# Softmax reciprocals by way of HBM, a planner that serves transfers in turn, and a finer last tail, in a 32-graph GNN kernel

## The chip, the cores and the metric

The program runs on one core of a Trainium2 chip. The metric is the device time of one execution in microseconds (us), lower is better; three executions of the kernel before are known, and one more under the profiler.

## The reference

There are 32 independent graphs of 512 nodes with 256 features and a dense 512 x 512 adjacency matrix each. Every graph goes through four layers, and each layer ends with `x = layernorm(x + layer(x))`:

- **Layer 0**, attention with 8 heads of 32 features: `q, k, v = x@Wq+bq, x@Wk+bk, x@Wv+bv`; `scores = q k^T / sqrt(32)`, set to -9e15 where `adj` is not positive; `softmax` over the keys; `attn @ v`; `@ Wo + bo`.
- **Layer 1**: `h = (1+eps) x + adj@x`, then `relu(h@W1+b1)@W2+b2` with 512 hidden features.
- **Layer 2**: `eps x + adj@x`, `@W1+b1` with 1024 hidden features, RMS norm, silu, `@W2+b2`.
- **Layer 3**: a layer norm with gamma and beta, a degree-normalised Laplacian `L = I - D^-1/2 adj D^-1/2`, `softplus(xn@W_self + L@xn@W_neigh)`.

All of it is in float32. The division of the softmax by its row sums is what the first part of the change is about: for each head and each query there is one row sum, and the attention output (features on the partitions, queries along the free dimension) has to be multiplied by its reciprocal.

## The kernel before, in words

**Tiles.** P is 128 partitions and NT = 4 row tiles make one graph. Two groups `g` of four heads each (HPG = 4) are worked on at a time. For each row tile `t` TensorE (PE) writes four score matrices to `sc` (L779); VectorE (DVE) adds the mask and takes the row minimum (L803); ScalarE (ACT) takes exp and adds up the row sums `rs` (L817); DVE transposes the 1 MB tile `pq` in 32 x 32 blocks (L853); four DMAs carry it to a scratch tensor `via` in HBM (L865) and one carries it back as `pT`, now fully transposed (L877). After four tiles PE multiplies by `v` (L895, `po_att`), and the result goes to `oT`.

**The softmax reciprocals** (`normalise`, stage `rinv`). DVE takes the reciprocal of the 128 x 32 row sums into `rv` (L954). `split` turns it into three bf16 parts (three casts L919, two subtractions L926), PE transposes the parts (`pm_t`, L936), DVE or ACT copies the result to `mT` (L943, L944), and for each head group four bf16 matmuls with the 0/1 selector `sel_r` write the reciprocals, spread over the 32 features of each head, to the PSUM bank `pr_r` (L965). DVE multiplies `oT` by it (L976). `split` is used a second time for the RMS norm of layer 2 (`pb`, L1316).

**The dense stages** after it are `po<-wo` (L993), `ph` (aggregation, L1172), `pa` and `pg` (first dense layers, L1189), `po<-w` (second dense layers, L993), `pz` (L1438) and `pa_l` (Laplacian, L1480). The aggregated rows are held in `hT`, a tile with one buffer; the tag `xT`, with one buffer too, holds `xT` and later in the same graph `xnT` (the transposed input of layer 3). `adjT` has two buffers, `pq` two, `pT` four. `xT`, `adjT` and `xnT` are loaded from HBM in blocks with 128-byte pieces (`load_blocks`, L590) and finished by a DVE transpose (L677, L624, L1423). The last graph takes PE transposes for `xnT` and works in two halves (`row_tiles`).

**The order.** Nothing is left to queues at run time: every operation of all 32 graphs is put into a list with its engine, a cost in ns, what it reads and writes and which buffers it takes; `Order.run` plays a list scheduler over it and `Order.emit` issues the instructions of each engine in the order found. At each step the engine whose next operation could start first goes, and of the operations that it could start within 100 ns the one with the smallest key goes: `b * PERIOD + due + LEAD[stage]`, where `due` is a time from a schedule of one graph alone and LEAD a hand-set shift for each stage; the last graph has `HASTE` taken off. All DMAs go through SyncE's queue (SP), which issues in that order and waits in order. Before the change the planner lets a DMA take its cost from its own issue on, however many others are under way:

```
free[e] = o.t1 - self.TAIL[e] if e != "SP" else t + way[3].get("issue", 100)
```

so that SP is taken for the `issue` time alone, and the costs are long (6500 and 7500 ns for the 1 MB to and from `via`, 4900 for one of four `xT` blocks, 5800 for one of four `adjT` blocks).

**The end of the last graph** (stage `softplus`): softplus is computed as max(z,0) + ln(1 + exp(-|z|)). For each half ACT takes |z| (L1515), exp (L1520, after a table load) and ln (L1533, after a table load); DVE adds; the layer norm and the store follow.

Of the kernel before, what the change touches and what calls it, by code (L numbers as in the profile page):

```python
# [9 lines left out]
F32 = mybir.dt.float32  # L10
BF16 = mybir.dt.bfloat16
AF = mybir.ActivationFunctionType
ALU = mybir.AluOpType
# [3 lines left out]
P = 128  # L17
# [2 lines left out]
RMS_EPS = 1e-6  # L20
HEADS = 8

PERIOD = 63146
LEAD = {
    "adjT": 62300, "agg1": -7100, "agg2": -126300, "degree": 48800, "diag": 69400, "lap": -8500,
# [4 lines left out]
}  # L30


# [27 lines left out]
class Order:  # L60
# [9 lines left out]
    TABLE, TABLE_DUE = 1300, 9000  # L70

    TURN = {"whole": 93, "row": 290, "col": 150}
    TURN_DUE = 1750
    LATE = 0.17
    HASTE = -6727

    def __init__(self):
        self.ops = []
# [29 lines left out]
    def run(self, ops, key, back=False):  # L108
# [22 lines left out]
        table, turn = [None], ["whole"]  # L131

        pool_busy, dve_busy = [0.0, 0.0], [0.0, 0.0]

        def add(o):
            for i, way in enumerate(o.ways):
# [18 lines left out]
        while len(out) < len(ops):  # L155
# [67 lines left out]
                    if lst[i][2] is o:  # L223
                        del lst[i]
            o.t0, o.t1, o.way = t, t + cost, way
            free[e] = o.t1 - self.TAIL[e] if e != "SP" else t + way[3].get("issue", 100)
            end = o.t1 + way[3].get("lat", self.LAT[e])
            for x in o.bufs:
                if not x.taken:
# [53 lines left out]
def kernel(  # L283
# [68 lines left out]
        return sel  # L352

    NX = 2 * NT * HPG
    sel_r = selector(NX, HD, "sel_r")
    sel_t = selector(NT, P, "sel_t")


# [11 lines left out]


    def setup(engine, cost, fn, r=(), w=()):
        order.op(-1, [(engine, cost, fn, {"issue": cost})], r, w, (), None)

    def load(name, t, src, kb):
        setup("SP", max(560, kb * 2.8), lambda: nc.sync.dma_start(t, src), (), [(name,)])

    def load_w(w, name):
        k, m = w.shape
# [21 lines left out]
    def load_x(b, t):  # L401
        nc.sync.dma_start(t(), x[b].rearrange("(t p) d -> p t d", p=P))

    def load_adj(b, t):
        nc.sync.dma_start(t(), adj[b].rearrange("(t p) j -> p t j", p=P))
# [102 lines left out]
    def graph(b):  # L508
# [60 lines left out]
        def small(name, bufs=2, shape=None):  # L569
            return Buf(sb, shape or [P, NT], F32, "s_" + name, f"{name}_{b}", bufs)  # L570
# [3 lines left out]
        y = tmp([P, NT, D], "y_att", 2)  # L574
        ad = Buf(sb, [P, NT, N], F32, "adj_sb", f"adj_{b}", 1)
        op(
            [("SP", 4000 if first else 8100, lambda: load_x(b, y), {"issue": 1500 if first else 560, "lat": 300})],
            [], [(y, t) for t in range(NT)],
        )
        op(  # L580
            [("SP", 6000 if first else 8900, lambda: load_adj(b, ad), {"issue": 3000 if first else 560, "lat": 300})],
            [], [(ad, t) for t in range(NT)],
        )

# [9 lines left out]
        if early:  # L594
            for m in range(NT):
                pt = bank("pt_adj")

                def tr_adj(m=m, pt=pt):
                    for t in range(NT):
                        nc.tensor.transpose(  # L600
                            pt[:, t * P : (t + 1) * P], ad[:, t, m * P : (m + 1) * P], ident
                        )

                pe(
                    460, tr_adj, [(ad, t) for t in range(NT)],
                    [(pt,), ("began", m)], adjT, d_out,
                )
                act(
                    675,
                    lambda m=m, pt=pt: nc.scalar.activation(  # L610
                        adjT[:, m, :], pt(), AF.Identity, accum_out=d_out[:, m : m + 1]
                    ),
                    [(pt,)], [(adjT, m), (d_out, m)],
                )
        else:
            for q in range(4):
                op(
                    [("SP", 5800, lambda q=q: load_blocks(adjT(), adj[b], q), {"issue": 1250, "lat": 300})],
                    [("began", m) for m in range(NT)], [(adjT, m, q) for m in range(NT)],
                )  # L620
            for m0 in range(0, NT, 2):
                dve(
                    1200,
                    lambda m0=m0: nc.vector.transpose(  # L624
                        adjT[:, m0 : m0 + 2].rearrange("p m i -> p (m i)"),
                        adjT[:, m0 : m0 + 2].rearrange("p m i -> p (m i)"),
                    ),
                    [], [(adjT, m, q) for m in range(m0, m0 + 2) for q in range(4)]
                    + [(adjT, m) for m in range(m0, m0 + 2)],
                )  # L630
            for m in range(NT):
                act(
                    675,
                    lambda m=m: nc.scalar.activation(
                        adjT[:, m, :], adjT[:, m, :], AF.Identity, accum_out=d_out[:, m : m + 1]
                    ),
                    [], [(adjT, m), (d_out, m)],
                )
# [30 lines left out]
        else:  # L669
            for q in range(4):  # L670
                op(
                    [("SP", 4900, lambda q=q: load_blocks(xT(), x[b], q), {"issue": 660, "lat": 300})],
                    [("begun", c) for c in range(DC)], [(xT, c, q) for c in range(DC)],
                )
            dve(
# [89 lines left out]
        def attend(g):  # L765
# [5 lines left out]
            for t in range(NT):  # L771
# [78 lines left out]
                else:  # L850
# [12 lines left out]
                    def away(pq=pq, via=via):  # L863
                        for i in range(4):
# [3 lines left out]
                            )  # L868

                    op(  # L870
                        [("SP", 6500, away, {"issue": 2240, "lat": 300})],
                        [(pq, j) for j in range(HPG)], [(via,)],
                    )
                    op(
                        [(
                            "SP", 7500,
                            lambda pT=pT, via=via: nc.sync.dma_start(  # L877
                                pT().rearrange("p i j c s -> p (i j c s)"),
                                via().rearrange("a p i e -> (a p) (i e)"),
                            ),  # L880
                            {"issue": 600, "lat": 300},
                        )],
                        [(via,)], [(pT, a) for a in range(4)],
                    )
# [62 lines left out]

        def normalise():

            stage[0] = "rinv"  # L950
            rv = small("rv", 2, [P, NX])
            dve(
                240,
                lambda: nc.vector.reciprocal(rv(), rs().rearrange("p g t j -> p (g t j)")),  # L954
                [(rs, g, t, j) for g in range(2) for t in range(NT) for j in range(HPG)],
                [(rv,)],
            )
            mT = split(rv, NX, "sums")
            for g in range(2):
                pr_r = bank("pr_r")  # L960

                def spread(g=g, pr_r=pr_r):
                    for t in range(NT):
                        x = (g * NT + t) * HPG
                        nc.tensor.matmul(  # L965
                            pr_r[:, t * P : (t + 1) * P],
                            lhsT=sel_r[0 : 3 * NX, x : x + HPG].rearrange("p j e -> p (j e)"),
                            rhs=mT[0 : 3 * NX],
                            start=True,
                            stop=True,  # L970
                        )

                pe(240, spread, [(mT,)], [(pr_r,)])
                dve(
                    700,
                    lambda g=g, pr_r=pr_r: nc.vector.tensor_tensor(  # L976
                        oT[:, g, :], pr_r(), oT[:, g, :], ALU.mult
                    ),
                    [(pr_r,)], [(oT, g)],
                )  # L980

        def pair_sum(lhs, lhs_k, w, w_k, nk, y, step):
# [418 lines left out]
        else:  # L1401
            x3d = Buf(dr, [N, D], F32, "x3d", f"x3d_{b}", 2)
            op(
                [(
                    "SP", 6000,
                    lambda: nc.sync.dma_start(
                        x3d().rearrange("(t p) d -> p t d", p=P), x3()
                    ),
                    {"issue": 560, "lat": 300},
                )],  # L1410
                [(x3, t) for t in range(NT)], [(x3d,)],
            )
            for q in range(4):
                op(
                    [(
                        "SP", 4900, lambda q=q: load_blocks(xnT(), x3d(), q),
                        {"issue": 660, "lat": 300},
                    )],
                    [(x3d,)], [(xnT, c, q) for c in range(DC)],
                )  # L1420
# [83 lines left out]
        for rt in row_tiles:  # L1504
# [6 lines left out]
            s_ = lambda part=part: sp[:, part]  # L1511
            z_ = lambda part=part: zy[:, part, 0:D]
            x_ = lambda part=part: x3[:, part]
            act(
                cost, lambda s_=s_, z_=z_: nc.scalar.activation(s_(), z_(), AF.Abs), z0,  # L1515
                spk + [("sp", b)],
            )
            act(
                cost,
                lambda s_=s_: nc.scalar.activation(s_(), s_(), AF.Exp, scale=-1.0), [], spk,  # L1520
                table="exp",
            )

            dve(
                100 + 275 * n,
# [13 lines left out]
        for rt in row_tiles:  # L1539
            part = slice(rt[0], rt[-1] + 1)  # L1540
            op(
                [(
                    "SP", 3000,
                    lambda part=part: nc.sync.dma_start(
                        out[b].rearrange("(t p) d -> p t d", p=P)[:, part], sp[:, part]
                    ),
                    {},
                )],
                [(sp, t) for t in rt], [("out", b, rt[0])],
            )  # L1550
# [45 lines left out]
```

## Time and profile before

| | |
|---|---|
| median of 3 runs | 3408.11 us |
| lowest and highest | 3400.85 and 3408.37 us |
| the profiled execution's own time | 3402.63 us |
| its span, first to last instruction | 3400.9 us |
| granted TensorE clock | 0.993 |
| PE busy | 3305.0 us (97%) |
| DVE, ACT, POOL busy | 2751.4 (81%), 1897.9 (56%), 843.0 (25%) us |
| DMA queue of SP | 673.71 MB, packets 73.1% of 16 engines' span |

Busy times are sums over one core. Matmuls are pipelined and their modelled ends overlap, so PE's time for a step is read from the chain of waits (what released what, in order of time) rather than from the mean of one instruction. "SPq" is the SP queue that issues DMAs, and a piece of it on the chain is time in which the next transfer could not be issued yet. The times of the steady part repeat from graph to graph at 103.4 us: the aggregation of the fourth graph starts at 406.7 us and that of the thirtieth at 3094.9.

### The profile page before, as it was taken

To read this page: it belongs to the slowest core of one execution; us is meant where nothing else is said; L and a number is where in the kernel's file an instruction comes from. 1 tells how busy PE (TensorE), PEld (TensorE's weight loads), DVE (VectorE), ACT (ScalarE), POOL (GpSimd) and SP (SyncE) were. 2 spreads that over 40 slices of the span, in tenths; PEclk is the share of its full clock that TensorE was granted. 3 is DMA by queue.
4 is the path that set the end of the run, shared out by engine and by line. 5 is a ranking of instruction groups with operands and counts; after the bars stand their busy time and mean duration, and the time that the engine had idled before them with its cause. 6 is when DMAs were issued, how large, how long until landed. Compare 5 with 4: busy or idle time off the path is not lost.

```text
span 3400.9 us, 54937 instructions
## 1 busy us (share of the span) xinstructions
PE 3305.0 (97%) x19624; PEld 1992.9 (59%) x19624; DVE 2751.4 (81%) x6338; ACT 1897.9 (56%) x3936; POOL 843.0 (25%) x610
## 2 busy tenths in 40 slices
PE   8999999999999999999999999999999999999997
PEld 5556665566665566555665655665555666556554
DVE  8778888888888878887788888788888788887855
ACT  6455565555665555655555655556555556555523
POOL 1222222222222222223222223222222222222221
PEclk9999999999999999999999999999999999999999
DMA  6777877777877777777778777778777787776820
GB/s 161 222 230 196 244 199 220 190 218 205 226 199 224 181 222 203 209 217 190 215 210 222 199 223 184 220 205 217 215 212 193 214 215 198 223 191 189 218 37 13
DMA packets 768194, 677.22 MB, mean 199 GB/s; under 512 B 540208, under 2 KB 592304, under 8 KB 736176
## 3 DMA queue, kind: packets, MB, share of 16 engines
q1 hardware_dynamic: 767920, 673.71, 73.1%
q8 instruction: 155, 2.54, 0.3%
q14 instruction: 119, 0.97, 0.1%
HBM read 380.52 MB, written 293.08 MB: 198 GB/s over the span
## 4 chain that ended last, share of the span: by engine, by line
PE 69%; DMA 12%; SPq 11%; DVE 5%; issue 2%; ACT 1%; DVEq 0%; POOL 0%; POOLq 0%; ACTq 0%
PE ph L1172 13%; PE pg L1189 13%; PE po L993 10%; SPq L590 10%; PE pq L706 6%; DMA pT<-via 6%; PE sc L779 6%; PE pa L1189 6%; DMA adjT<-in_adj_dram 4%; PE po_att L895 4%; PE pz L1438 4%; PE pv L747 3%; PE pa_l L1480 2%; DVE pq L853 2%; DVE adjT L624 1%
## 5 line engine op out<-in xcount | busy, mean ns | idle before, releaser
L817 ACT ACTIVATE pq<-pq,mx 128x512 f32<-128x512 f32 x1024 | 727.6, 712 | 266.5 <-DVE mx L803 207.6
L803 DVE CUSTOM_DVE_ANT_0 pq<-sc,bias 128x512 f32<-128x512 f32 x1024 | 654.3, 682 | 39.0 <-PE sc L779 23.3
L853 DVE STREAM_TRANSPOSE pq<-pq 128x2048 f32<-128x2048 f32 x248 | 568.7, 2293 | 30.2 <-ACT pq L817 29.9
L993 PE MATMUL po<-w,gT 128*128 128x256 f32 x2048 | 458.1, 382 | 6.3 <-ACT gT L1343 6.3
L1189 PE MATMUL pg<-hT,w 128*128 128x512 f32 x1024 | 460.7, 598 | 0.0
L993 PEld LDWEIGHTS po<-w,gT 128*128 128x128 f32 x2048 | 388.5, 191 | 77.7 <-issue 19.5
L549 POOL TENSOR_TENSOR ssq<-ssq,sq 128x512 f32<-128x512 f32 x217 | 277.0, 1276 | 599.6 <-ACT sq L1265 599.6
L1046 POOL TENSOR_TENSOR rstd<-ve,nhalf 128x4 f32<-128x4 f32 (+1 forms) x132 | 136.6, 1035 | 1013.9 <-DVE ve L1041 1012.2
L1189 PEld LDWEIGHTS pg<-hT,w 128*128 128x128 f32 x1024 | 189.4, 190 | 260.8 <-issue 251.1
L779 PE MATMUL sc<-kT,qT 32*128 32x512 f32 x2048 | 293.7, 643 | 9.2 <-DVE mx L803 9.2
L895 PEld LDWEIGHTS po_att<-pT,v 128*32 128x32 f32 x8192 | 220.1, 110 | 53.6 <-issue 26.2
L1438 PE MATMUL pz<-wsn,xnT 128*128 128x512 f32 x512 | 242.8, 609 | 4.2 <-DVE gT L1244 4.2
L895 PE MATMUL po_att<-pT,v 128*32 128x128 f32 x8192 | 238.3, 274 | 4.6 <-DMA pT<-via 4.6
L1480 PE MATMUL pa_l<-zy,adjT 128*128 128x256 f32 x1024 | 242.4, 385 | 0.0
L1172 PE MATMUL ph<-adjT,y 128*128 128x512 f32 x512 | 231.3, 605 | 6.6 <-DVE y L1064 3.9
L1172 PE MATMUL ph<-adjT,y_att 128*128 128x512 f32 x512 | 229.0, 600 | 7.5 <-issue 7.5
L993 PE MATMUL po<-w,aT 128*128 128x256 f32 x1024 | 229.5, 382 | 0.2 <-DVE aT L1213 0.2
L1189 PE MATMUL pa<-hT,w 128*128 128x512 f32 x512 | 225.3, 593 | 0.0
L993 PEld LDWEIGHTS po<-w,aT 128*128 128x128 f32 x1024 | 192.1, 190 | 47.9 <-issue 21.0
L1480 PEld LDWEIGHTS pa_l<-zy,adjT 128*128 128x128 f32 x1024 | 189.4, 190 | 29.8 <-issue 0.7
L1328 DVE SCALAR_TENSOR_TENSOR gT<-gT,rw_c,pb 128x512 f32<-128x512 f32 x256 | 171.3, 742 | 35.0 <-PE pb L1316 35.0
L817 ACT ACTIVATION_READ_ACCUMULATOR pq<-pq,mx 128x1 f32 x1024 | 191.9, 187 | 0.0
(165 smaller groups left out, 4686.7 us busy)
## 6 DMA issues: line engine op xcount, KB each, us to landing
via<-pq SPq DMA_DIRECT2D x992, 256.0 KB, 4.4
pT<-via SPq DMA_DIRECT2D x248, 1024.0 KB, 7.8
adj<-in_adj_dram SPq DMA_DIRECT2D x32, 1024.0 KB, 5.4
adjT<-in_adj_dram SPq DMA_DIRECT2D x124, 256.0 KB, 6.4
y_att<-in_x_dram SPq DMA_DIRECT2D x32, 512.0 KB, 6.3
xT<-in_x_dram SPq DMA_DIRECT2D x124, 128.0 KB, 6.2
x3d<-y SPq DMA_DIRECT2D x31, 512.0 KB, 4.4
xnT<-x3d SPq DMA_DIRECT2D x124, 128.0 KB, 3.8
```

What stands on the lines that cost most here:

```text
L549: lambda: nc.gpsimd.tensor_tensor(dst(), dst(), src(), ALU.add), {},
L590: nc.sync.dma_start(dst[32 * q : 32 * q + 32].rearrange("r m (i c) -> r m i c", c=32), v[q])
L779: nc.tensor.matmul(sc[:, j, :], lhsT=qT[hp, g, t * P : (t + 1) * P], rhs=kTs[g][hp, :], start=True, stop=True,)
L803: lambda t=t, j=j, sc=sc, row=row: nc.vector.tensor_tensor_reduce(out=row(), in0=sc[:, j, :].rearrange("p (a n) -> p a n", a=4), in1=bias[ ...
L817: lambda t=t, j=j, row=row: nc.scalar.activation(row(), row(), AF.Exp, bias=mx[:, t, j : j + 1], scale=-1.0, accum_out=rs[:, g, t, j : j + 1],
L853: lambda pq=pq: nc.vector.transpose(pq().rearrange("p a j c s -> p (a j c s)"), pq().rearrange("p a j c s -> p (a j c s)"),),
L895: nc.tensor.matmul(po[j * HD : (j + 1) * HD, t * P : (t + 1) * P], lhsT=v[:, c, h * HD : (h + 1) * HD], rhs=pTs[t][:, :, j, c, :], start=( ...
L993: nc.tensor.matmul(po[:, i * D : (i + 1) * D], lhsT=lhs[:, k, t * P : (t + 1) * P], rhs=w[:, k, :], start=(i == 0 and k == 0), stop=(i == ...
L1172: nc.tensor.matmul(ph(), lhsT=xin[:, m, c * P : (c + 1) * P], rhs=adjT[:, m, :], start=(m == 0), stop=(m == NT - 1),)
L1189: nc.tensor.matmul(pa(), lhsT=w[:, c, m * P : (m + 1) * P], rhs=hT[:, c, :], start=(c == 0), stop=(c == DC - 1),)
L1438: nc.tensor.matmul(pz(), lhsT=xnT[:, c, t * P : (t + 1) * P], rhs=wsn[:, c, :], start=(c == 0), stop=(c == DC - 1),)
L1480: nc.tensor.matmul(pa[:, i * D : (i + 1) * D], lhsT=adjT[:, m, t * P : (t + 1) * P], rhs=zy[:, m, D : 2 * D], start=(m == 0), stop=(m == N ...
```

## The change

1. The reciprocals no longer go over PE. DVE takes the reciprocal and transposes `rv` in 32 x 32 blocks; four DMAs write it to an HBM scratch `rd` (32 x 128 numbers, 16 KB); four DMAs read it back with a broadcast over 32 partitions each, into `of` (512 KB), which takes the one buffer of the tag `hT`; DVE multiplies `oT` by `of` from SBUF. `sel_r`, the split, the PE transpose and the spreading matmuls of this step go.
2. The planner serves transfers one after the other: a DMA ends its cost after the one before it has ended. The costs become transfer times (2750 for 1 MB by `via`, 1250 for an `xT` block, 2500 for an `adjT` block) and 2000 ns from its end to the readiness of its data. PERIOD, the table LEAD, TURN_DUE, LATE and HASTE have new values, so the order of all instructions changes.
3. In the last graph |z| and exp are issued for one row tile at a time instead of two; ln stays in halves.

The diff, its core:

```diff
-PERIOD = 63146
+PERIOD = 71820
 LEAD = {
-    "adjT": 62300, "agg1": -7100, "agg2": -126300, "degree": 48800, "diag": 69400, "lap": -8500,
-    "ln0": -32000, "ln1": -86500, "ln2": 24300, "ln3": -8000, "load": -81700, "move": 3000,
-    "pv": 15200, "pz": 25500, "qk": 3900, "rinv": -46700, "rms": -136300, "scores": -5800,
-    "silu": 7600, "softplus": -22800, "v": -39700, "w11": -91100, "w12": -41600, "w21": 11000,
-    "w22": -3300, "wo": 45900, "x3T": 53600, "xT": 13300,
+    "adjT": -200, "agg1": 2900, "agg2": -52500, "degree": -8900, "diag": 53900, "lap": 20400,
+    "ln0": 500, "ln1": -55000, "ln2": 115600, "ln3": 22300, "load": -13700, "move": -2100,
+    "pv": 49500, "pz": 17500, "qk": 42000, "rinv": -5700, "rms": -10400, "scores": -12400,
+    "silu": -39000, "softplus": 34200, "v": -37700, "w11": -2000, "w12": 2000, "w21": -34700,
+    "w22": -3600, "wo": -14900, "x3T": -3700, "xT": -41100,
 }
...
-    TURN_DUE = 1750
-    LATE = 0.17
-    HASTE = -6727
+    TURN_DUE = 1000
+    LATE = 0.01
+    HASTE = -14532
...
-            free[e] = o.t1 - self.TAIL[e] if e != "SP" else t + way[3].get("issue", 100)
+            if e == "SP":
+
+                n, issue = way[3].get("n", 1), way[3]["issue"]
+                moved = o.t1 = max(max(t + issue / n, moved) + cost, t + issue + cost / n)
+            free[e] = o.t1 - self.TAIL[e] if e != "SP" else t + way[3]["issue"]
...
-                    [("SP", 5800, lambda q=q: load_blocks(adjT(), adj[b], q), {"issue": 1250, "lat": 300})],
+                    [("SP", 2500, lambda q=q: load_blocks(adjT(), adj[b], q), {"issue": 1250})],
...
-                    [("SP", 4900, lambda q=q: load_blocks(xT(), x[b], q), {"issue": 660, "lat": 300})],
+                    [("SP", 1250, lambda q=q: load_blocks(xT(), x[b], q), {"issue": 660})],
...
-                        [("SP", 6500, away, {"issue": 2240, "lat": 300})],
+                        [("SP", 2750, away, {"issue": 2240, "n": 4})],
...
-                            "SP", 7500,
+                            "SP", 2750,
...
         def normalise():
 
+
             stage[0] = "rinv"
             rv = small("rv", 2, [P, NX])
+
+            def turned():
+                nc.vector.reciprocal(rv(), rs().rearrange("p g t j -> p (g t j)"))
+                nc.vector.transpose(rv(), rv())
+
             dve(
-                240,
-                lambda: nc.vector.reciprocal(rv(), rs().rearrange("p g t j -> p (g t j)")),
+                440, turned,
                 [(rs, g, t, j) for g in range(2) for t in range(NT) for j in range(HPG)],
                 [(rv,)],
             )
-            mT = split(rv, NX, "sums")
+            rd = Buf(dr, [NX, P], F32, "rd", f"rd_{b}", 2)
+            of = tmp([P, 2, NT, P], "hT", 1, "of")
+
+            def away():
+                for i in range(4):
+                    nc.sync.dma_start(
+                        rd[:, 32 * i : 32 * i + 32], rv[32 * i : 32 * i + 32, :]
+                    )
+
+            def back():
+                v = rd().rearrange("(gt j) q -> j gt q", j=HPG)
+                for j in range(HPG):
+                    nc.sync.dma_start(
+                        of[j * HD : (j + 1) * HD].rearrange("p g t q -> p (g t) q"),
+                        v[j].partition_broadcast(HD),
+                    )
+
+            op(
+                [("SP", 400, away, {"issue": 2240, "n": 4})],
+                [(rv,)], [(rd,)],
+            )
+            op(
+                [("SP", 2200, back, {"issue": 2240, "n": 4})],
+                [(rd,)], [(of,)],
+            )
             for g in range(2):
-                pr_r = bank("pr_r")
-
-                def spread(g=g, pr_r=pr_r):
-                    for t in range(NT):
-                        x = (g * NT + t) * HPG
-                        nc.tensor.matmul(
-                            pr_r[:, t * P : (t + 1) * P],
-                            lhsT=sel_r[0 : 3 * NX, x : x + HPG].rearrange("p j e -> p (j e)"),
-                            rhs=mT[0 : 3 * NX],
-                            start=True,
-                            stop=True,
-                        )
-
-                pe(240, spread, [(mT,)], [(pr_r,)])
                 dve(
                     700,
-                    lambda g=g, pr_r=pr_r: nc.vector.tensor_tensor(
-                        oT[:, g, :], pr_r(), oT[:, g, :], ALU.mult
-                    ),
-                    [(pr_r,)], [(oT, g)],
+                    lambda g=g: nc.vector.tensor_tensor(
+                        oT[:, g, :], of[:, g].rearrange("p t q -> p (t q)"), oT[:, g, :], ALU.mult
+                    ),
+                    [(of,)], [(oT, g)], port=True,
                 )
...
-            act(
-                cost, lambda s_=s_, z_=z_: nc.scalar.activation(s_(), z_(), AF.Abs), z0,
-                spk + [("sp", b)],
-            )
-            act(
-                cost,
-                lambda s_=s_: nc.scalar.activation(s_(), s_(), AF.Exp, scale=-1.0), [], spk,
-                table="exp",
-            )
+            for u in [(t,) for t in rt] if last else [rt]:
+                su = lambda u=u: sp[:, u[0] : u[-1] + 1]
+                zu = lambda u=u: zy[:, u[0] : u[-1] + 1, 0:D]
+                suk = [(sp, t) for t in u]
+                act(
+                    200 + 215 * len(u),
+                    lambda su=su, zu=zu: nc.scalar.activation(su(), zu(), AF.Abs),
+                    [(zy, t, 0) for t in u], suk + [("sp", b)],
+                )
+                act(
+                    200 + 215 * len(u),
+                    lambda su=su: nc.scalar.activation(su(), su(), AF.Exp, scale=-1.0), [], suk,
+                    table="exp",
+                )
```

What is cut are the same kinds of edits at the remaining DMAs (a transfer time for the cost, the 2000 ns of latency for the 300, an `issue` of 560 where there was none) and the line that built `sel_r`.

More of the change, by code (lines that the diff above doesn't have):

```diff
@@ L133, in run @@
         pool_busy, dve_busy = [0.0, 0.0], [0.0, 0.0]
+        moved = 0.0
         def add(o):
@@ L354 @@
     NX = 2 * NT * HPG
-    sel_r = selector(NX, HD, "sel_r")
     sel_t = selector(NT, P, "sel_t")
@@ L372, in setup @@
     def setup(engine, cost, fn, r=(), w=()):
-        order.op(-1, [(engine, cost, fn, {"issue": cost})], r, w, (), None)
+        order.op(-1, [(engine, cost, fn, {"issue": 560})], r, w, (), None)
     def load(name, t, src, kb):
-        setup("SP", max(560, kb * 2.8), lambda: nc.sync.dma_start(t, src), (), [(name,)])
+        setup("SP", kb * 2.6, lambda: nc.sync.dma_start(t, src), (), [(name,)])
     def load_w(w, name):
@@ L576, in graph @@
         op(
-            [("SP", 4000 if first else 8100, lambda: load_x(b, y), {"issue": 1500 if first else 560, "lat": 300})],
+            [("SP", 1330, lambda: load_x(b, y), {"issue": 560})],
             [], [(y, t) for t in range(NT)],
@@ L580, in graph @@
         op(
-            [("SP", 6000 if first else 8900, lambda: load_adj(b, ad), {"issue": 3000 if first else 560, "lat": 300})],
+            [("SP", 2650, lambda: load_adj(b, ad), {"issue": 560})],
             [], [(ad, t) for t in range(NT)],
@@ L880, in attend @@
                             ),
-                            {"issue": 600, "lat": 300},
+                            {"issue": 600},
                         )],
@@ L1404, in graph @@
                 [(
-                    "SP", 6000,
+                    "SP", 1330,
                     lambda: nc.sync.dma_start(
@@ L1408, in graph @@
                     ),
-                    {"issue": 560, "lat": 300},
+                    {"issue": 560},
                 )],
@@ L1415, in graph @@
                     [(
-                        "SP", 4900, lambda q=q: load_blocks(xnT(), x3d(), q),
-                        {"issue": 660, "lat": 300},
+                        "SP", 1250, lambda q=q: load_blocks(xnT(), x3d(), q),
+                        {"issue": 660},
                     )],
@@ L1542, in graph @@
                 [(
-                    "SP", 3000,
+                    "SP", 1330,
                     lambda part=part: nc.sync.dma_start(
@@ L1546, in graph @@
                     ),
-                    {},
+                    {"issue": 560},
                 )],
```

## The prediction

> **What bounds the kernel now.** I read the busy lines of the page first, then busy time by stretch, PE's waits in the steady part, the chain of waits over one graph, and last the rows of what the change removes.
>
> ```profile
> PE 3305.0 (97%) x19624; PEld 1992.9 (59%) x19624; DVE 2751.4 (81%) x6338; ACT 1897.9 (56%) x3936; POOL 843.0 (25%) x610
> PE 69%; DMA 12%; SPq 11%; DVE 5%; issue 2%; ACT 1%; DVEq 0%; POOL 0%; POOLq 0%; ACTq 0%
> ```
>
> PE is busy for 97% of the span, yet the chain runs on PE for only 69% of it: a quarter goes over transfers and the queue that issues them, although PE is working then. By stretch (us, then PE, PEld, DVE, ACT, POOL busy, clock, DMA share, GB/s; start, the 26 steady graphs, end):
>
> ```profile
> 0.00:406.70 406.70, 376.96 (x2537) 228.26 (x2537) 329.64 (x767) 230.55 (x524) 85.22 (x65) 0.98 0.76 208
> 406.70:3094.90 2688.20, 2653.64 (x15804) 1597.94 (x15805) 2222.31 (x5096) 1543.18 (x3197) 691.97 (x495) 1.00 0.77 209
> 3094.90:3400.90 306.00, 274.35 (x1283) 166.71 (x1283) 199.47 (x477) 124.14 (x216) 65.84 (x52) 0.96 0.40 101
> ```
>
> PE idles 29.7 us at the start, 34.6 us over 26 graphs (1.3 of each 103.4), and 31.7 at the end. In the steady part nearly all of that is one wait (total, times, longest):
>
> ```profile
> PE pv L747 <- DVE xT L677: 27.2, 23, 2.8
> PE ph L1172 <- issue: 5.4, 24, 0.2
> ```
>
> Where it comes from, the chain over one graph shows (start, length, what):
>
> ```profile
> 2195.53 7.06 PE ph L1172 x16
> 2202.60 0.45 PE pr_r L965 x8
> 2203.05 1.07 PE sc L779 x8
> ...
> 2228.72 0.87 PE pz L1438 x2
> 2229.59 8.96 DMA pT<-via
> 2238.55 0.02 issue
> 2238.56 5.62 SPq L590
> ...
> 2254.41 6.21 DMA pT<-via
> 2260.62 1.19 DVE adjT L624
> 2261.81 2.19 DVE pq L853
> 2264.00 1.14 DVE xT L677
> 2265.14 0.04 issue
> 2265.18 3.72 PE pv L747 x16
> ...
> 2293.00 5.15 PE pq L706 x12
> 2298.15 0.06 PE pm_t L936
> ```
>
> From 2229.59 to 2265.18, 35.6 us, the end is set by a row of transfers (`pT`, four blocks of `xT`, four of `adjT`, `pT` again) and three DVE transposes; PE has other work for 34 of them and then waits. The two steps that the change takes off PE, `pr_r` and `pm_t`, lie outside this stretch, on PE's own part of the chain. That is the whole case for a gain, and the stretch is the case against it.
>
> **PE loses two steps per graph.** By the rows, 19.6 us of busy time for `pr_r` and 7.1 for `pm_t` go in all, (19.6 + 7.1)/32 = 0.83 us a graph. Matmuls overlap their neighbours, so the chain is the better price: 0.45 + 0.06 = 0.51. Bounds 0.51 and 0.83; I take 0.51, as the chain already leaves out the overlap: 32 x 0.51 = 16.3 us (26.6 at most).
>
> **DVE** loses per graph three casts, two subtractions and a copy (rows 148 + 2 x 191, 182 + 192, 214 ns: 1.12 us) and gains a 128x32 transpose. Transposes of 2048, 1024 and 512 columns take 2293, 1225 and 709 ns, about 0.2 us and 1 ns a column, so 0.2 us here by the line through them. The two multiplications stay: 680 ns from PSUM, 692 for an addition of that size from SBUF (`sp`, L553). The sum is 0.9 us less, on an engine with 17% to spare and no place on PE's path here: nothing. What could come back shows in two rows (ns, least, median, most):
>
> ```profile
> L976 DVE TENSOR_TENSOR oT<-pr_r,oT x64: 650/680/692, 70.5 to 3257.2; 128x512 f32<-128x512 f32 x64
> L1154 DVE TENSOR_TENSOR adjT<-diag,self x64: 649/686/1229, 48.3 to 3292.9; 128x512 f32<-128x512 f32 x64
> ```
>
> With one operand in PSUM the longest is the median; with both in SBUF one took 0.54 us longer. Even if each of the 64 did, it is 35 us over 32 graphs, and with POOL busy for 25% rather 9, all on DVE's spare time. I count nothing. The Trainium skill (SBUF - State Buffer, Who interferes with whom) speaks against the change here: a VectorE instruction with two SBUF inputs contends with a GpSimd instruction that reads SBUF, and the later one waits to the end. By that rule each hit could cost the rest of one 1.28 us addition of POOL, some 10 us of DVE in all (an estimate), which leaves the sum as it is.
>
> **SP and the transfers.** Eight more issues a graph. A group of four to `via` takes SP 2.85 us when nothing holds it, four from `x3d` 3.00, so 5.85 of 103.4 us for both groups. SP's three longest waits alone are 944.9 + 199.3 + 122.2 = 1266 us, 37% of the span, so its total is no bound. The read back waits, in SP's order, until the write has landed: `via` writes land in 4.4 us (2.6 to 13.7), and whatever is queued behind waits too, next tiles' `via` writes above all, for which a freed `pq` buffer and then scores wait. The planner can set other issues between write and read; the trace shows SP doing that for `pT`, with 199.3 us of waits over 248 reads, 0.8 each. The new bytes, 512 KB a graph, are priced by the queue's own speed: 673.71 MB in 73.1% of 3400.9 us is 271 GB/s, 1.9 us. Bounds: 1.3 us by the longest pieces and 5.6, half of the 11.3 us that SP took over four `xT` blocks when held up. I take 2. Where it lies decides. Outside the stretch above it costs nothing, since PE waits for no transfer there. Between the row sums of a graph (`rv` at 2289.7) and its use in `wo` (2235.3 in the graph before, so 2338.7) lie 49 us, enough for write and read (2.85 + 4.4 + 3 + some 4 to 8 us of landing). But `of` needs the one `hT` buffer, which the traced order leaves free only for 14 us between the two aggregations and from 2222.3 (end of `pg`) to 2269.1 (next `ph`), and the second of these covers the stretch. `hT` itself is held 15.7 + 26.8 us a graph, with `of` some 54 of 103: not a bound by its length.
>
> **The planner's prices.** Before, it expects `adjT` to be there 12.5 us after the first `xT` issue (four times 660, three times 1250, 5800 and 300). In the trace the first `xT` is issued at 2236.1 and the transposes of `adjT` start at 2259.4: 23 us. The new prices give 4 x 1.25 + 4 x 2.5 + 2 = 17 us, and 22.5 with two tile moves of 2.75 in front, near what is seen. So the plan that follows can put real cover where PE now runs dry, and the shifts move the loads forward (`xT` by 54 us, `adjT` by 62, in units of the key). That reaches at most the 34.6 us of steady idle. Against it stands that every other placement changes too, `ln2` is put back by 91 us, `aT`/`zy` and `xT`/`xnT` share single buffers, and PE at 99% in the steady part can lose more than it can win. Bounds: -34.6 and +60 (2 us a graph, the size of today's longest wait of that kind, 2.8); I take -4, little more than nothing, because the page prices no order.
>
> **The tail.** ACT runs without a gap from 3385.0 to 3393.9 through both halves: |z| 0.63, table 1.28, exp 0.63, table 1.28, ln 0.63. Row by row, two more instructions of each half cost about 0.2 us each (some 0.8 in all) and the first starts 0.44 earlier; if exp of a third tile goes before the first ln, two tables (2.56 us) are saved. Between +0.4 and -2.6; I take 0. **The start** loses one selector, 0.7 us of DVE, while PE waits for a load: nothing.
>
> **Sum.** 3402.6 (profiled, span 3400.9) - 16.3 - 4 - 0 = 3382; the median shown is 5.5 us above the profiled run and two of the three are near it, so I add some 2: 3384.
>
> **The rivals.**
>
> *The read back falls into the transfer stretch (slower).* Place: between the end of `pg` and the next `pv`, where `hT` is free and transfers already end 1.5 us after PE's work. Price: 2.0 to 4 us of transfer and issue that reach PE whole; over 29 graphs 58 to 116, less 16: 3444 to 3502, about 3460. It decides from 0.51 us a graph, where the saving is used up. For it: the chain and the `hT` tag. Against: the planner now sees transfers in turn, and moves the loads.
>
> *The freed time turns into waits (no change).* Another order, 0.5 us more idle a graph: 3398 to 3408. For it: a quarter of the chain runs over transfers, and these don't shrink. Against: the removed steps are on PE's part.
>
> *The order also closes the steady waits (faster still).* 3402.6 - 26.6 - 27 to 34 = 3341 to 3349, if late loads were the only cause and the new order has no waits of its own. For it: one wait is 27.2 of 34.6 us. Against: it would be PE at 100%.
>
> **How the numbers follow.** A difference under 0.3% (10 us) can't be told from none here. Forecast (3368 to 3397) 0.46, faster still 0.14, no change 0.11, slower 0.29. Faster is 0.60, same 0.11, slower 0.29. The range leaves some 0.05 below and 0.14 above: 3342 to 3458.
>
> **What would show it.** Right: no `pr_r` rows, PE's busy time down by 16 to 27 us, a period near 102.8, `pv` waiting less for `xT`. The first rival: `pv` or `wo` waits in each graph for a transfer of `of` or for a load behind it, and the period is over 104. Wrong altogether: waits over 3 us a graph at a place that is quiet today, or start and end together over 75 us idle instead of 61.

## The result and the profile after

The changed kernel takes 3384.31 us (median of 4 runs, 3382.35 to 3388.02) against 3404.48 us for the kernel before on the same chip: ratio 0.9942, 95% interval 0.9924 to 0.9961. A second comparison on another chip gave 0.9954 (0.9941 to 0.9966). The number that was predicted, 3384, was met, but by luck, as the experiments below show. One term of the sum was right; two were far off, in opposite directions, and cancel.

The page of the changed kernel, busy lines and the chain by engine:

```profile
PE 3288.6 (97%) x19336; PEld 1977.0 (58%) x19336; DVE 2715.8 (80%) x6150; ACT 1927.6 (57%) x3968; POOL 840.2 (25%) x610
q1 hardware_dynamic: 808880, 691.03, 79.2%
PE 80%; DMA 10%; DVE 4%; SPq 3%; issue 1%; ACT 1%; POOL 0%; POOLq 0%; DVEq 0%; ACTq 0%
```

PE's busy time fell by 16.4 us, 0.51 us a graph as forecast (to the digit by chance, as the two orders differ: runs 1 and 12 below, with the same planner and shifts, are 17.5 us apart); the span fell by 20.3, so idle time fell by only 3.9 (95.9 to 92.0). By stretch, cut at the same two graphs as before (columns as before):

```profile
0.00:408.30 408.30, 374.99 (x2374) 227.62 (x2375) 318.18 (x722) 223.81 (x499) 85.65 (x65) 0.97 0.74 199
408.30:3077.80 2669.50, 2644.47 (x15576) 1585.02 (x15575) 2190.06 (x4941) 1567.84 (x3225) 689.15 (x494) 1.00 0.84 216
3077.80:3380.60 302.80, 269.16 (x1390) 164.32 (x1388) 207.54 (x489) 135.91 (x246) 65.42 (x51) 0.96 0.49 124
```

A steady graph now takes 2669.5/26 = 102.67 us instead of 103.39. PE still idles 25.0 us in that stretch; but it is another wait. PE's waits in it (total, times, longest):

```profile
PE pm L1302 <- DVE red L1294: 24.9, 21, 3.5
```

The wait of `pv` for `xT` (27.2 us) is gone altogether. In the kernel before, DVE came late to the transpose of `xT` because it stood idle for the loads of `adjT`, whose transposes are ahead in its order (DVE's wait: total, times, longest):

```profile
DVE adjT L624 <- DMA adjT<-in_adj_dram: 124.9, 29, 6.1
```

In the changed kernel that wait is 2.6 us. But the new wait, of the small RMS matmul `pm` for the reduction `red` on DVE, wasn't there before. The chain of waits over one graph shows what stands behind `red`:

```profile
2082.50 13.95 PE pg L1208 x32
2096.44 0.02 issue
2096.46 0.30 SPq L979
2096.76 0.04 issue
2096.81 1.55 SPq L979
2098.36 0.04 issue
2098.40 1.72 SPq L979
2100.12 0.04 issue
2100.17 4.24 DMA of<-rd
2104.40 0.02 issue
2104.43 0.69 DVE oT L995
2105.12 0.61 DVE red L1294
2105.73 0.04 issue
2105.77 0.40 PE pm L1302 x2
```

`pg` ends, SP issues the four reads back (L979), they land, DVE can multiply `oT` (L995), and `red`, which has nothing to do with it but is queued behind the multiplication on DVE, comes late for PE. The rows of the tile `of` say the same from DVE's side (its engine sat idle until; total us, times):

```profile
  DMA of<-rd: 38.0, 26
  ACT oT L546: 23.9, 28
```

DVE waited 38.0 us in 26 graphs for the read back, and PE waited 24.9 us for `red` in the steady part. Runs 4 and 12 below take the read back's lateness away, and PE's wait goes with it.

### The profile page after: what moved, and what is told of

Read it like the earlier page. It is cut to its first block, busy times and chain, and to the rows that moved or that the text cites. A ratio compares the mean times of both kernels' runs of the same rounds, so it can differ in the third digit from the quotient of the medians.

```text
span 3380.6 us, 54443 instructions
## 1 busy us (share of the span) xinstructions
PE 3288.6 (97%) x19336; PEld 1977.0 (58%) x19336; DVE 2715.8 (80%) x6150; ACT 1927.6 (57%) x3968; POOL 840.2 (25%) x610
## 3 DMA queue, kind: packets, MB, share of 16 engines
q1 hardware_dynamic: 808880, 691.03, 79.2%
## 4 chain that ended last, share of the span: by engine, by line
PE 80%; DMA 10%; DVE 4%; SPq 3%; issue 1%; ACT 1%; POOL 0%; POOLq 0%; DVEq 0%; ACTq 0%
PE po L1012 23%; PE ph L1191 11%; PE pg L1208 7%; PE po_att L899 7%; PE sc L783 7%; PE pa_l L1499 7%; PE pa L1208 6%; PE pq L710 6%; DMA of<-rd 3%; PE pv L751 3%; DMA pT<-via 3%; DMA via<-pq 2%; PE pz L1457 1%; DMA xnT<-x3d 1%; DVE pq L807 1%
## 5 line engine op out<-in xcount | busy, mean ns | idle before, releaser
L807 DVE CUSTOM_DVE_ANT_0 pq<-sc,bias 128x512 f32<-128x512 f32 x1024 | 674.3, 684 | 95.9 <-PE sc L783 73.0
L1012 PE MATMUL po<-w,gT 128*128 128x256 f32 x2048 | 466.2, 384 | 13.1 <-ACT gT L1362 12.1
L1208 PE MATMUL pg<-hT,w 128*128 128x512 f32 x1024 | 448.0, 595 | 0.0
L1263 DVE TENSOR_SCALAR gT<-pg,b_c 128x512 f32<-128x512 f32 x191 | 143.2, 751 | 131.6 <-PE pg L1208 131.4
L1012 PE MATMUL po<-w,aT 128*128 128x256 f32 x1024 | 238.5, 387 | 0.0
L1284 ACT ACTIVATE sq<-gT 128x512 f32<-128x512 f32 x224 | 140.5, 627 | 167.8 <-POOL ssq L553 162.0
L1457 PE MATMUL pz<-wsn,xnT 128*128 128x512 f32 x512 | 225.7, 592 | 0.3 <-DVE xnT L1411 0.3
```

Of the source, the lines that this page charges most:

```text
L807: lambda t=t, j=j, sc=sc, row=row: nc.vector.tensor_tensor_reduce(out=row(), in0=sc[:, j, :].rearrange("p (a n) -> p a n", a=4), in1=bias[ ...
L1012: nc.tensor.matmul(po[:, i * D : (i + 1) * D], lhsT=lhs[:, k, t * P : (t + 1) * P], rhs=w[:, k, :], start=(i == 0 and k == 0), stop=(i == ...
L1208: nc.tensor.matmul(pa(), lhsT=w[:, c, m * P : (m + 1) * P], rhs=hT[:, c, :], start=(c == 0), stop=(c == DC - 1),)
L1457: nc.tensor.matmul(pz(), lhsT=xnT[:, c, t * P : (t + 1) * P], rhs=wsn[:, c, :], start=(c == 0), stop=(c == DC - 1),)
```

## The experiments

Idle time below is the span less PE's busy time. The kernels of one set ran on one chip beside the kernel before (medians 3398.5, 3403.33 and 3398.97 us in the three sets), so ratios are compared between sets.

**1. The order without the reciprocals' new way.** The changed kernel with the `normalise` of before put back, in short:

```diff
+    sel_r = selector(NX, HD, "sel_r")
...
-            op([("SP", 400, away, {"issue": 2240, "n": 4})], [(rv,)], [(rd,)])
-            op([("SP", 2200, back, {"issue": 2240, "n": 4})], [(rd,)], [(of,)])
+            mT = split(rv, NX, "sums")
...
+                pe(240, spread, [(mT,)], [(pr_r,)])
```

> The new planner, shifts and tail, with the reciprocals spread by PE as before (parts 2 and 3 without part 1). Theory A, PE's own work sets the time: the two steps come back at 0.51 us a graph, +16 us on the changed kernel's 3384, so about 3400. Theory B, the new order alone made the gain: about 3384. Theory C, PE's work counts and the read back costs the changed kernel its 24.9 us of waits (pm waiting for red): 3384 + 16 - 25, about 3375.

Measured: 3368.55 us, ratio 0.9912 (0.9898 to 0.9925). That is below the changed kernel, and nearest to theory C. Its page:

```profile
PE 3301.1 (98%) x19624; PEld 1989.7 (59%) x19624; DVE 2758.1 (82%) x6368; ACT 1899.9 (56%) x3913; POOL 841.6 (25%) x610
PE 93%; DVE 2%; DMA 1%; issue 1%; ACT 1%; SPq 1%; POOL 0%; POOLq 0%; DVEq 0%; ACTq 0%
```

The chain is on PE for 93% of the span (69% before), and over the 26 steady graphs, cut at the same two aggregations, PE never idles (busy by stretch):

```profile
417.44:3068.44 2651.00, 2651.00 (x15809) 1593.52 (x15808) 2226.87 (x5123) 1542.32 (x3173) 688.71 (x494) 1.00 0.81 212
```

DVE has no wait for `adjT` in it at all. So the new prices and shifts (with the tail's edit, which lies outside this stretch) gained all of the 34.6 us of steady idle time and 30 us in total; which of the two did it, no run separates. And the way by HBM, put on top, lost 0.3 to 0.4% again, 10 to 14 us by the two ratios of the changed kernel.

**2. The reciprocals' new way without the order.** The kernel before with the new `normalise`, prices in the old manner:

```diff
+                [("SP", 4800, away, {"issue": 2240, "lat": 300})],
+                [("SP", 7600, back, {"issue": 2240, "lat": 300})],
```

> Part 1 alone: the reciprocals by way of HBM with the planner, shifts and tail of before; the two new transfers get prices in the old manner (4800 and 7600 ns from the first issue, close to what the changed kernel's trace shows). Theory A: 3404 - 16, about 3388. Theory B, no gain without the new order: about 3404 or more. Theory C, the read back reaches PE by 1 us a graph or more where the old planner puts it: 3404 - 16 + 26 or more, 3414 up.

Measured: 3810.94 us, ratio 1.1216 (1.1201 to 1.1232), far beyond theories A and B. Theory C has no upper end, but its cause isn't there: PE's busy time is 3412.5 us and it idles 392.7, while DVE waits for the read back for only 7.6 us in all. Experiments 8 and 9 ask why.

**3. The price of the removed step.** In the kernel before:

```diff
-                    for t in range(NT):
+                    for t in [*range(NT), *range(NT), *range(NT)]:
                         x = (g * NT + t) * HPG
```

> The kernel before, with each of the eight spreading matmuls issued three times in a row (the same result written again) at the planner's old price, so nothing moves in the order. It prices the removed step by itself. By the chain (0.45 us per eight) two more sets cost 32 x 0.90 = 29 us, so 3433; by busy time (0.61) 39 us, 3443; if PE's waits swallow it, 3404.

Measured: 3432.47 us, ratio 1.0095 (1.0081 to 1.0109), 34 us more. A set of eight costs 34/64 = 0.53 us on the path (0.43 to 0.58 by the interval): the chain's 0.45 fits, the row's 0.61 doesn't. Idle time absorbs little of it (91.1 us against 95.9), and no other wait of PE moves by more than 3 us.

**4. Nobody waits for the read back.** The changed kernel, the same order and transfers:

```diff
-                        oT[:, g, :], of[:, g].rearrange("p t q -> p (t q)"), oT[:, g, :], ALU.mult
+                        oT[:, g, :], cb, oT[:, g, :], ALU.mult
```

> The changed kernel with the same order and the same transfers, but the two multiplications read a constant tile instead of the tile that the read back fills, so nothing waits for the read back (the division by the row sums is left out). If the read back, late by its landing, holds VectorE and through it the pm matmul, the 24.9 us of steady waits go: about 3359. If red is late by VectorE's own queue, they stay: about 3384.

Measured: 3346.06 us, ratio 0.9846 (0.983 to 0.986). The waits of `pm` are gone, 28.4 us down to 1.7 over the whole span, and idle time is 62.4 us. So the late read back cost the changed kernel 0.0096 to 0.0108 of 3400 us, 33 to 37 us, more than its 24.9 us of waits: PE's busy time falls too, by 9.9 us, and the last section shows why. The bytes themselves, which still move here, cost nothing to be seen: PE idles no longer than in run 1 (66.7 us).

**5. The changed kernel again**, beside the next three.

> The changed kernel once more, on the chip of the next three, to compare with them directly. About 0.994 of the kernel before, so 3378 to 3385.

Measured: 3383.99 us, ratio 0.9954 (0.9941 to 0.9966).

**6. A buffer of its own, order drawn again** (an unused constant goes to make room, here and in 8, 9, 11 and 12).

```diff
-            of = tmp([P, 2, NT, P], "hT", 1, "of")
+            of = tmp([P, 2, NT, P], "of", 1, "of")
```

> The changed kernel with a buffer of its own for the tile that the read back fills, in place of the one of hT (an unused constant goes, to make room). Theory D, the read back is late because it waits for the end of pg to get hT: the 24.9 us of pm waits go, and with 16 us less of PE work than the new order with PE's reciprocals (0.991 of before, 3369) it comes to 0.985 to 0.988, about 3350. Theory E, any way by HBM is late, whatever the buffer: 0.994, about 3380. A new order is drawn with it, which could cost some 10 us either way.

Measured: 3421.08 us, ratio 1.0054 (1.0041 to 1.0067): slower, not faster. The planner, with one constraint less, drew another order; `pm` waits 37.0 us in it and `pz` 19.3. By its time alone the experiment doesn't answer its question, because the order moved with the buffer. The traces tell more. PE's order differs from the changed kernel's in eight matmuls of the last graph only, and over the steady graphs the read back stands where run 12 below puts it by hand in SP's queue. But the planner also sets the first multiplication further forward on DVE, six places ahead of `red` instead of one, and DVE waits there (total us, times):

```profile
  DMA of<-rd: 154.4, 30
```

So the buffer can be free and the place in SP's queue early, and the kernel is slower still when the reader stands too early in its own queue.

**7. A later readiness told to the planner.**

```diff
-                [("SP", 2200, back, {"issue": 2240, "n": 4})],
+                [("SP", 2200, back, {"issue": 2240, "n": 4, "lat": 5000})],
```

> The changed kernel, with the planner told that the read back is ready 5000 ns after its transfer rather than 2000 (the trace shows 7.9 us from the first issue to the landing, the planner reckons 4.8). hT stays its buffer. If only the price was wrong, the planner puts other work on VectorE before the multiplications, the pm waits go and it takes 3355 to 3365; if the one buffer of hT is the matter, hT is held longer still and it stays at 3380 or gets slower.

Measured: 3485.66 us, ratio 1.0246 (1.0233 to 1.026). A price nearer to the trace made the order worse: `ph` waits 53.1 us for the layer norm in 27 graphs, `pm` still 26.0. The edit did what it was meant to: DVE never waits for the read back in this run. But the order moved again, and its other waits cost more; `red`, now ahead of the multiplication, is late for another reason that wasn't traced.

**8. and 9. Part 1 alone with its own buffer**, with the order drawn again (8) and kept to the instruction (9, the planner still reckoning with hT's buffer):

```diff
-            of = tmp([P, 2, NT, P], "hT", 1, "of")
+            of = tmp([P, 2, NT, P], "of", 1, "of")
+            of.slot = ("sb", "hT")            # 9 only: what the planner counts
```

> Part 1 alone in the order of before, which took 3811 us, with a buffer of its own for the tile that the read back fills. Theory D, the wait for hT at the head of SP's queue, with the loads of xnT and adj behind it, made the 412 us: most of it goes, 3385 to 3450. Theory E, the old planner's prices make any added transfer collide: 3600 and over.

> Part 1 alone (3811 us) with its order kept to the instruction and a buffer of its own for the tile that the read back fills. It tells how much of the 407 us is the wait for hT: theory D, SP's queue stands at hT with loads behind it, more than half of it goes, under 3600; theory F, the order that the old planner draws for the new list of operations is bad in itself, 3700 or more.

Measured: 3638.42 us (1.0696, 1.0681 to 1.0712) and 3812.17 us (1.1211, 1.1196 to 1.1225). With the order kept, the buffer is worth nothing, 3812 against 3811; so theory D falls, and the some 175 us between 8 and 9 came from the order that was drawn. The time of 8 lies in theory E's range, which doesn't show its cause. In 9, too, DVE waits little for the read back (8.8 us). That leaves theory F or the added transfers themselves in the old order; no run has the old order with the transfers put in.

**10. Another order and nothing else.** The kernel before:

```diff
-PERIOD = 63146
+PERIOD = 64146
```

> The kernel before with PERIOD 64146 instead of 63146, 1.6% more, and nothing else: the same work, another order drawn. If the settings are worth little, 3395 to 3415; if each order is a draw and the settings in the file were the good ones of many, it is slower by 30 us or more, and the 412 us of part 1 alone and the 37 and 101 us of the two redrawn ones are of that kind.

Measured: 3742.82 us, ratio 1.1011 (1.0997 to 1.1025), for the same work (74 copies moved from ACT to DVE). The busy line of its page, and PE's longest wait:

```profile
PE 3372.7 (90%) x19624; PEld 2022.0 (54%) x19624; DVE 2799.6 (75%) x6412; ACT 1870.3 (50%) x3862; POOL 849.3 (23%) x611
```

```profile
PE ph L1172 <- DVE adjT L1154: 165.9, 20, 15.1
```

A shift of one setting by 1.6% costs 344 us, nearly as much as part 1 alone in the old settings (412). So the times of runs 2, 6, 7 and 8 can't be read as prices of their edits: a draw of the order alone can cost that much. Which property of the drawn order is to blame is seen for run 6 (above); for 2, 7 and 8 it stays open.

**11. and 12. The order kept, the read back freed.** The changed kernel with the own buffer and `of.slot` as in 9 (11), and in addition the read back moved up by two places in SP's queue, ahead of four `via` writes and a `pT` read, after planning (12):

```diff
+        for o in [o for o in out if o.way[3].get("early")]:
+            i = out.index(o)
+            sp = [j for j in range(i) if out[j].way[0] == "SP"]
+            j = sp[-o.way[3]["early"]]
+            j = max([j] + [1 + k for k in range(i) if out[k].n in o.preds])
+            out.insert(j, out.pop(i))
...
+                [("SP", 2200, back, {"issue": 2240, "n": 4, "early": 2})],
```

> The changed kernel with every engine's order kept to the instruction, but the tile that the read back fills has its own buffer (the planner still reckons with hT's; one unused constant goes). SP then need not wait for the end of pg: 41.8 us of its waits, 1.5 a graph, go. Theory D, hT holds the read back: the pm waits of 24.9 us are 0.9 a graph, less than 1.5, so most of them go: 3384 down to 3360 to 3368. Theory E, SP's queue itself is late there: 3380 or more.

> As of_own_same, and the read back stands two places earlier in SP's queue, ahead of one pT read and four via writes; all other engines' orders are kept. It comes some 6 us earlier. If the late read back is all that the way by HBM costs, this comes to what the kernel took whose multiplications waited for nothing, 0.985 of before, 3350 to 3360, and beats the new order with PE's reciprocals (0.991). If the transfers set back behind it make PE wait instead, 3365 or more.

Measured: 3382.95 us (0.9953, 0.994 to 0.9966) for 11, no different from the changed kernel; 3348.66 us (0.9843, 0.983 to 0.9855) for 12. The SP waits before the read back (total, times, longest) show why 11 gave nothing; first the changed kernel, then run 11:

```profile
SPq L979 <- PE pg L1208: 41.8, 27, 2.9
SPq L979 <- DMA pT<-via: 12.3, 11, 2.2
```

```profile
SPq L978 <- DMA pT<-via: 44.3, 25, 2.8
SPq L978 <- DMA adj<-in_adj_dram: 7.7, 14, 0.9
```

Without the wait for `pg` the read back waits just as long for earlier transfers at the same place of the queue. In 12 its place differs, and everything else stands where it stood. Its page, the rows of `of`, and the issues of SP over that part of one graph (start, length, line, what):

```profile
PE 3283.6 (98%) x19336; PEld 1972.1 (59%) x19336; DVE 2708.1 (81%) x6149; ACT 1927.6 (58%) x3968; POOL 839.8 (25%) x610
```

```profile
  ACT oT L550: 19.2, 28
  DMA of<-rd: 0.5, 1
```

```profile
2071.01 3.43 SPq L977 DMA_DIRECT2D rd<-rv  x4
2074.55 2.90 SPq L873 DMA_DIRECT2D via<-pq  x4
2077.55 1.16 SPq L413 DMA_DIRECT2D adj<-in_adj_dram  x1
2078.82 3.24 SPq L984 DMA_DIRECT2D of<-rd  x4
2082.17 0.38 SPq L885 DMA_DIRECT2D pT<-via  x1
2082.60 5.05 SPq L873 DMA_DIRECT2D via<-pq  x4
```

DVE's wait for the read back falls from 38.0 us to 0.5 and the kernel takes what run 4 took, though it divides. The `pT` and `via` transfers set back behind it, by 3 us, don't hold PE: it has no idle time in the 26 steady graphs, which take 101.41 us each. This version beats both kernels.

## Why the prediction was right, and where it wasn't

The steady graph makes the account. Before: 103.39 us. With the new order and PE's reciprocals (run 1): 101.96 (2651.0/26). With the reciprocals by HBM and read in time (run 12): 101.41 (2636.7/26). The changed kernel: 102.67.

- **PE loses two steps** (forecast 0.51 us a graph, bounds 0.51 and 0.83). 101.96 - 101.41 = 0.55; run 3 has 0.53 for the spreading alone (0.43 to 0.58). Right, and for the reason given: the chain, and not the row's busy time, is near the price of a short step among overlapping ones.
- **The planner's prices** (forecast -4 us in all, bounds -34.6 and +60). 103.39 - 101.96 = 1.43 us a graph, 37 us over 26 graphs: the size was wrong by nearly all of the term, just past the end of the bounds, which I held for hardly reachable ("it would be PE at 100%"). PE is at 100% there. The evidence was in the prediction: nearly all of the steady idle time was one wait behind late loads, the old prices reckoned 12.5 us for them where 23 were seen, and the new ones 17 to 22.5. I set it nearly aside because every other placement changes too. What runs 2, 6, 7, 8 and 10 showed is that this caution was right about the risk, 37 to 412 us for a redrawn order, and that a value near nothing was a poor choice: orders differ by tens and hundreds of us, so the term was either most of the idle time or a large loss, hardly -4.
- **SP and the transfers** (forecast 0). 102.67 - 101.41 = 1.26 us a graph, 33 us over 26 graphs; runs 4 and 12 give 33 to 38 in all. Of the 33, 25 are PE's idle time and 8 its longer busy time. I had this as the first rival, at 2 to 4 us a graph, with its place right ("between the end of `pg` and the next `pv`") and its mechanism half right: the read back is late in SP's queue behind `pg`. But the loads behind it don't hold PE, and `hT` alone isn't the cause (run 11); its place in the queue makes DVE wait, and DVE's queue carries that to a matmul of another step. The question that I asked for SP, what is queued behind the waiting instruction, I didn't ask for DVE, where I had called the multiplications free for lack of load.
- **The bytes.** Priced at 1.9 us of transfer a graph. The queue's packets took 691.03 MB in 79.2% of 3380.6 us, 2677 us, against 76.4% of 3367.8, 2573, in run 1: 3.3 us a graph. That is 70% more than priced, and it costs PE nothing all the same (runs 4 and 12).
- **DVE** and the shared port. The transpose took 212 ns (forecast 0.2 us), the multiplications 693 (forecast 692), the longest 694: none of the 64 was held up by POOL. The rule of the Trainium skill on two SBUF inputs (SBUF - State Buffer, Who interferes with whom) cost nothing here, as the planner kept these instructions off POOL's long ones. Run 8 shows the rule at work, as the last section tells.
- **The tail** (0, bounds +0.4 and -2.6). ACT's last two halves run from 3364.18 to 3373.61, 9.43 us instead of 8.91; from the last Laplacian matmul to the end it is 13.5 us after and 13.4 before. Read from the trace only: 0.1 us can't be told apart by running it.

By the steady graph, -0.55 - 1.43 + 1.26 = -0.72 us, 19 us over 26 graphs, nearly all of the 20 that the span lost and that I had summed as -16 - 4 - 0. Two misses, of some 33 us each, cancelled: the number was luck, the first term wasn't. By the marks that the prediction set (no `pr_r`, 16 us less PE, a period near 102.8, no wait for `xT`) it looks right throughout. The marks of the first rival, as written, aren't met (`pv` and `wo` don't wait in the steady part, the period is under 104); its trace is one engine further up, in DVE's wait for `of` in 26 graphs.

## What to carry to other kernels

When an engine is busy for 97% and the chain is on it for only 69%, see first what the other queues make late: here a new order, in which no load is late, brought more than twice what taking work off PE did. The read back cost here by its place in SP's queue and by the place of its reader in DVE's, not by its bytes, and the wait that it caused travelled on through DVE's queue to steps that don't use its data. To test one edit in a kernel whose order comes from a planner, keep the order fixed to the instruction: of the six variants here that drew a new one, the times of four (2, 6, 7 and 8) don't price their edit.

## What the runs showed of the hardware

**The granted clock answers to idle time**, so a bad order costs twice. In the kernel with only PERIOD changed the steady stretch ran at 0.96 (us, then PE, PEld, DVE, ACT, POOL busy, clock, DMA share, GB/s):

```profile
400.00:3200.00 2800.00, 2542.53 (x14855) 1523.88 (x14854) 2121.14 (x4835) 1419.69 (x2934) 645.48 (x458) 0.96 0.72 188
```

PE's busy time rose from 3305.0 to 3372.7 us for the same matmuls; the clock records show 0.5 in stretches of 3.4 us and multiples of it, 8.9% of the span there, 11.7% in part 1 alone (granted clock 0.942) and 1.5% in the kernel before. The Trainium skill (TensorE: Matmul & The Clock Gate, Part 1) says that the clock falls to half after an idle window of about 3.4 us; the length of the stretches agrees with it, but the window need not be idle throughout. Cut into pieces of 3.4 us in step with the clock records, this run has 36 pieces after which the clock fell, and PE idled for 1.8 to 3.4 us in each; in the other 957 at full clock it idled for 1.7 us at most. In run 7 PE's longest gap in the steady part is 2.4 us, and the clock fell 25 times there. This is also why the late read back cost more than its waits: the steady part of the changed kernel has 13.7 us at half clock and those of runs 4 and 12 none, which is worth some 7 of the 8 us of longer busy time.

**Two SBUF inputs on DVE.** In run 8, 14 of the 64 multiplications by `of` took 0.92 to 1.78 us instead of 0.69. Each began while POOL was at an addition of 512 columns or more, and each ended 0.55 us after that addition did. Small instructions of POOL (128x4) running beside such a multiplication didn't lengthen it.
